# Attention scores of one block as single-pass products of exact float32r halves

## The chip, the cores and the metric

The kernel runs on one core of a Trainium2 chip. The metric is the device time of one execution in microseconds (us). Half a per cent of it is about 27 us.

## The reference, cut to what matters

The input is x (8 sequences of 512 tokens, 256 features) and a context of the same shape. Four residual blocks follow one another: an mLSTM cell over the context, block 2 with attention and experts, block 3 with cross attention, block 4 with a product-key expert layer. The change is in block 2's attention, 32 heads of 8 features each:

```python
xn = (x - mu) / jnp.sqrt(var + 1e-05) * ln_g + ln_b
q = (xn @ wq).reshape(B, S, H, hd)          # H = 32, hd = 8
k = (xn @ wk).reshape(B, S, H, hd)
v = (xn @ wv).reshape(B, S, H, hd)
att = jnp.einsum('bqhd,bkhd->bhqk', q, k) / np.float32(np.sqrt(hd))
p = jax.nn.softmax(att, axis=-1)
o = jnp.einsum('bhqk,bkhd->bqhd', p, v).reshape(B, S, D) @ wo + x
```

Block 3's attention is of the same kind with 16 heads of 16 features. All of it is float32.

## The kernel before

**Phases.** `attention_phase` holds blocks 1 to 3, sequence by sequence (136 to about 3432 us in the trace below), `scores_phase` the queries and key scores of block 4, and the rest of the kernel block 4's experts. The change is in the first phase alone.

**Attention jobs.** There are 24 jobs of 16 heads each: for each of the eight sequences m two jobs of block 2, ("A", m, 0) and ("A", m, 1), which share out its 32 heads, and one of block 3, ("C", m, 0). They run in the order A0 A1 of sequence 0, then for each next m A0, A1 and C of m - 1, at last C of the last (L698). Each job has two passes of 16 steps, and each step two halves:

- *maxima* (L274): for two heads, scores of 128 queries against all 512 keys go to PSUM (`sc`, two banks), and DVE reduces them to the negated maximum (L282). After 16 steps `close_maxima` (L288) transposes the maxima, and four DMAs write them into row 17 of each head's 32-row group of `qa`.
- *exponentials* (L302): the same scores the other way round, keys on the partitions. Row 17 of `ka` is all ones, so the product already has the maximum subtracted. ACT takes the exponential (L310); a step later `values` (L316) multiplies it with v (L324).

`qa` and `ka` are [128, 4, 512]: four row groups of 32 partitions, one for each of four heads that TensorE works on side by side, and four such sets g. Of the 32 rows a block 2 head uses 8 (features) and row 17; the other rows of ka are zero. There are three pairs, two for block 2 (f = 0, 1) and one for block 3. `pair` (L259) issues a product for each of two row groups (L265).

**Order of the work.** The main loop (L798) pairs, in each half, a maxima step of one job with an exponentials step of an earlier one, and issues the products in turn: maxima, exponentials, maxima, exponentials. A job's exponentials begin at least LAG = 2 ticks after its maxima are closed. The two share PSUM through `ps_sc` with two buffers, so that the next maxima products wait for DVE's L282, and the next exponentials for ACT's L310. After each half, `beside` (L774) lets two lanes of other work go on, up to a credit of 1.25 per half; what they yield is their estimated cost. Lane 1 does per sequence the loads, the cell (L379), `queries` (L525) and `values0`; lane 2 the experts, block 3's `operands` and `values1`, and `leave`. The framework may move instructions within each engine's stream by its own estimate; each engine then works in that order.

**Queries and keys of block 2.** `queries` normalises, transposes to `nT`, and projects (L536) into PSUM. ACT scales queries by 1/sqrt(8) (L539), DVE copies keys (L541). The results go to DRAM (`qk_d`, L542) and come back by `spread` (L233): four DMAs of 64 KB for each of qa and ka, each to 8 partitions. `blank` (L242) sets row 17 of qa to zero. Both wait until the previous sequence's job with the same f is done ("rest"). These DMAs go out on SP's queue, as do the maxima's (L298), the cell's `nM_d` (L424) and `mb` (L445), and x's stores.

**Start.** POOL fills the three pairs of qa and ka (L159, L160), then v0, v1 and cte, and then issues the first loads (L363). SP writes the rows of ones into ka (L168).

Of the kernel before, what the change touches and what calls it, by code (L numbers as in the profile page):

```python
# [9 lines left out]

F32 = mybir.dt.float32
U32 = mybir.dt.uint32
U16 = mybir.dt.uint16
U8 = mybir.dt.uint8
# [6 lines left out]
P = 128  # L21
# [13 lines left out]
def kernel(  # L35
# [65 lines left out]
    def attention_phase(ctx: ExitStack):  # L101
# [50 lines left out]

        sets = []
        for i in range(3):
            qa = cst.tile([P, 4, S], F32, name=f"qa{i}")
            ka = cst.tile([P, 4, S], F32, name=f"ka{i}")
            nc.gpsimd.memset(qa, 1.0)  # L159
            nc.gpsimd.memset(ka, 0.0)  # L160
            sets.append((qa, ka))
        ones_d = drm.tile([4, S], F32, name="ones_d", bufs=1)
        nc.sync.dma_start(ones_d.rearrange("(o g) s -> o g s", o=1), sets[0][0][0:1])
        zero_d = drm.tile([4, S], F32, name="zero_d", bufs=1)
        nc.sync.dma_start(zero_d.rearrange("(o g) s -> o g s", o=1), sets[0][1][0:1])
        for i in range(3):
            for j in range(4):
                nc.sync.dma_start(  # L168
                    sets[i][1][32 * j + 17 : 32 * j + 18, :, :],
                    ones_d.rearrange("(o g) s -> o g s", o=1),  # L170
                )


        W0, W1, WC = 32 * 9 + 23, 16 * 17 + 15, 8 * 33 + 31
# [7 lines left out]

        m_u8 = cst.tile([B * NC, P], U8, name="m_u8")
        nc.sync.dma_start(m_u8, mask)
        m_f = cst.tile([B * NC, P], F32, name="m_f")
        nc.vector.tensor_copy(m_f, m_u8)
        mp = ps_m.tile([P, S], F32, name="mp", tag="m")
        nc.tensor.transpose(mp[:, : B * NC], m_f, ident[: B * NC, : B * NC])
# [53 lines left out]
        def blank(qa):  # L242

            for j in range(4):
                nc.sync.dma_start(
                    qa[32 * j + 17 : 32 * j + 18, :, :],
                    zero_d.rearrange("(o g) s -> o g s", o=1),
                )

        class Attention:
            def __init__(self, m, qa, ka, va, first, hd):
                self.m, self.qa, self.ka, self.va = m, qa, ka, va
                self.first, self.hd = first, hd
                self.o = None

            def pair(self, lhs, rhs, g, c, jj):  # L259

                sc = ps_sc.tile([P, 2, S], F32, name="sc", tag="sc")

                def product(i):
                    r = 32 * (2 * jj + i)
                    nc.tensor.matmul(  # L265
                        sc[:, i, :],
                        lhs[r : r + 32, g, c * P : (c + 1) * P],
                        rhs[r : r + 32, g, :],
                        start=True, stop=True,
                    )  # L270

                return sc, product

            def maxima(self, n, half):  # L274

                g, c = n // NC, n % NC
                if n == 0 and half == 0:
                    self.nm = small.tile([P, NC, 4, 4], F32, name="nm")
                sc, product = self.pair(self.qa, self.ka, g, c, half)

                def then():
                    nc.vector.tensor_reduce(  # L282
                        self.nm[:, c, 2 * half : 2 * half + 2, g], sc, AX.X, ALU.max, negate=True
                    )

                return product, then

            def close_maxima(self):  # L288
                nmT = ps_m.tile([P, S], F32, name="nmT", tag="m")
                for c in range(NC):  # L290
                    nc.tensor.transpose(
                        nmT[:16, c * P : (c + 1) * P],
                        self.nm[:, c].rearrange("p j g -> p (j g)"), ident,
                    )
                nm_sb = row.tile([16, S], F32, name="nm_sb")
                nc.any.tensor_copy(nm_sb, nmT[:16])
                for j in range(4):
                    nc.sync.dma_start(  # L298
                        self.qa[32 * j + 17 : 32 * j + 18, :, :], nm_sb[4 * j : 4 * j + 4, :]
                    )  # L300

            def exponentials(self, n, half):  # L302
                g, c, jj = n // NC, n % NC, 1 - half
                if half == 0:
                    self.pr = [None, None]
                sc, product = self.pair(self.ka, self.qa, g, c, jj)

                def then():
                    self.pr[jj] = prb.tile([P, 2, S], F32, name="pr", tag="pr")
                    nc.scalar.activation(self.pr[jj], sc, AF.Exp)  # L310
                    if half == 1:
                        self.ready = (n, self.pr)

                return product, then
# [64 lines left out]
        def cell(m):  # L379
# [30 lines left out]
            nc.scalar.activation(e, e, AF.Exp, scale=-1.0)  # L410
            nc.scalar.activation(e, e, AF.Ln, bias=1.0)
            nc.vector.scalar_tensor_tensor(z, z, 0.0, e, ALU.min, ALU.subtract)
            cs = row.tile([8, S], F32, name="cs")
            nc.vector.tensor_tensor_scan(
                cs, ones[:8, 0:1].to_broadcast([8, S]), z, 0.0, ALU.mult, ALU.add
            )
# [108 lines left out]
        def queries(m):  # L525
            xn = tok.tile([P, NC, D], F32, name="xn", tag="t1")
            lnx[m] = layernorm(xn, xbs[m], keep=3)
            yield 0.3
            layernorm(xn, xn)
            yield 0.3  # L530
            nT = nTs[m] = trp.tile([P, NK, S], F32, name="nT", tag="nT")
            yield from to_features(nT, xn, affine=True)
            pds = [drm.tile([D, S], F32, name="qk_d", bufs=4) for _ in range(2)]
            for i in range(2):
                for n in range(NK):
                    ps = project_T(w0_sb[:, i], nT, n)  # L536
                    pk = trp.tile([P, S], F32, name="pk", tag="pk", bufs=2)
                    if i == 0:
                        nc.scalar.mul(pk, ps, 1.0 / math.sqrt(8.0))  # L539
                    else:  # L540
                        nc.vector.tensor_copy(pk, ps)  # L541
                    nc.sync.dma_start(pds[i][n * P : (n + 1) * P], pk)  # L542
                    yield 1.8
            for f in range(2):
                yield ("rest", ("A", m - 1, f))
                for i in range(2):
                    spread(sets[f][i], pds[i], 32 * f, 8)
                blank(sets[f][0])
                ready.add(("A", m, f))

        def values0(m):
# [75 lines left out]
        def operands(m):  # L627
# [5 lines left out]
            yield 0.3  # L633
            nT = trp.tile([P, NK, S], F32, name="nT3", tag="l2")
            yield from to_features(nT, xn)
            q1, k1 = sets[2]
            for i, srcT, dst in ((1, cT, k1), (0, nT, q1)):
                pd = drm.tile([D, S], F32, name="qk_d3")
                for n in range(NK):
# [148 lines left out]
        def operator(job):  # L788
            kind, m, f = job
            if kind == "A":  # L790
                return Attention(m, *sets[f], v0, 32 * f, 8)
            return Attention(m, *sets[2], v1, 0, 16)

        live, closed = {}, {}
        steps = [(job, n) for job in jobs for n in range(16)]
# [2 lines left out]
        while i2 < len(steps) or pending:  # L798
# [15 lines left out]
            for half in range(2):  # L814
# [2 lines left out]
                    work.append(live[one[0]].maxima(one[1], half))  # L817
                if two:
                    work.append(live[two[0]].exponentials(two[1], half))
                for i in range(2):  # L820
                    for product, _ in work:
                        product(i)
                for _, then in work:
                    then()
                if half == 0 and pending:
# [312 lines left out]
```

## Time and profile before

| | us |
|---|---|
| time, median of 3 runs | 5445.48 (5443.02 to 5463.35) |
| span of the profiled execution, first to last instruction | 5446.6 |
| PE busy in the span | 4895.7 (90%) |
| DVE busy | 2645.6 (49%) |
| ACT busy | 1768.4 (32%) |
| score products (L265), the two directions, PE busy | 1188.9 and 1029.3 |
| maxima (L282), DVE busy | 936.4 |
| exponentials (L310), ACT busy | 781.9 |

PE is TensorE's matmul, PEld its weight load, DVE VectorE, ACT ScalarE, POOL GpSimd, SP SyncE, which here only issues DMAs. A group's line gives the source line, the engine, the operation, output and inputs, shape and count, then busy time and the mean of one in ns, then the idle time just before them and what ended it. The chain is the work that ended last, followed back from the end, each step to what released it. PEclk is the granted clock of TensorE, as a share of full speed; its record knows full and half alone here. The profile gives no time of that execution beside the span.

### The profile page before, as it was taken

The numbers are of one execution on the slowest core, as the hardware profiler recorded it, in microseconds if no ns is written. First come the engines' busy times: TensorE is split into PE (matmuls) and PEld (weight loads), VectorE is DVE, ScalarE is ACT, GpSimd is POOL, SyncE is SP. The second block draws the span as 40 slices with busy tenths as digits, with TensorE's granted clock in tenths as the row PEclk, the third lists the DMA queues.
The fourth block names the chain that finished last, engine by engine and source line by source line (L and its number), as shares of the span: only waits on it lengthen the run. The fifth ranks groups of instructions, "written<-read, shape, count | busy, mean of one in ns | idle before, by whom it ended". The sixth has DMA issues, their size and how long they took to land.

```text
span 5446.6 us, 66461 instructions
## 1 busy us (share of the span) xinstructions
PE 4895.7 (90%) x27301; PEld 2702.6 (50%) x27301; DVE 2645.6 (49%) x5993; ACT 1768.4 (32%) x2314; POOL 232.0 (4%) x321
## 2 busy tenths in 40 slices
PE   6977898888888898888888788799999999999999
PEld 2322333223223233233233232466888888888888
DVE  3443344454453454454454413377855555555543
ACT  2133433344444344344344341355211111111110
POOL 3000010000000000000000000000000000000000
PEclk6688988789889889899889996899888888888887
DMA  2100011100101101111111001200111111111110
GB/s 82 31 17 5 28 50 44 32 28 21 47 25 35 44 28 37 36 32 36 32 24 40 16 17 24 99 1 5 61 45 55 42 53 51 40 58 43 43 52 10
DMA packets 96044, 200.24 MB, mean 37 GB/s; under 512 B 11310, under 2 KB 25934, under 8 KB 95246
## 3 DMA queue, kind: packets, MB, share of 16 engines
q1 hardware_dynamic: 79356, 142.69, 9.1%
q0 software_dynamic: 13056, 46.16, 2.7%
q10 hardware_dynamic: 3328, 7.13, 0.4%
q8 instruction: 215, 3.52, 0.3%
q14 instruction: 89, 0.73, 0.0%
HBM read 165.64 MB, written 29.52 MB: 36 GB/s over the span
## 4 chain that ended last, share of the span: by engine, by line
PE 77%; DVE 12%; issue 4%; DMA 3%; ACT 3%; POOL 1%; SPq 0%; POOLq 0%; DVEq 0%; ACTq 0%
PE sc L265 22%; PE cf L1059 10%; DVE nm L282 9%; PE ps_hd L1032 9%; PE acc L1070 9%; PE av L324 5%; PE ps_pq L883 4%; PE ps_sim L906 2%; PE csc L478 2%; PE ps_p L217 2%; PE ps_y L614 2%; PE ps_q L227 2%; PE cav L455 2%; PE ps_h L595 2%; PE ps_t L201 1%
## 5 line engine op out<-in xcount | busy, mean ns | idle before, releaser
L265 PE MATMUL sc<-ka,qa 32*128 32x512 f32 x3072 | 1188.9, 749 | 313.8 <-DVE nm L282 296.9
L282 DVE TENSOR_REDUCE nm<-sc 128x2 f32<-128x1024 f32 x768 | 936.4, 1223 | 979.4 <-PE sc L265 971.2
L310 ACT ACTIVATE pr<-sc 128x1024 f32<-128x1024 f32 x768 | 781.9, 1023 | 1196.6 <-PE sc L265 1194.6
L265 PE MATMUL sc<-qa,ka 32*128 32x512 f32 x3072 | 1029.3, 734 | 24.1 <-ACT pr L310 11.2
L265 PEld LDWEIGHTS sc<-ka,qa 32*128 32x128 f32 x3072 | 326.2, 211 | 927.7 <-DVE nm L282 759.5
L1032 PE MATMUL ps_hd<-xT,dw 128*128 128x256 f32 x2048 | 573.4, 440 | 14.0 <-ACT gs L1036 7.6
L1059 PEld LDWEIGHTS cf<-m,m 64*128 64x128 f32 x8192 | 560.4, 220 | 35.8 <-issue 31.1
L1059 PE MATMUL cf<-m,m 64*128 64x32 f32 x8192 | 571.9, 302 | 4.0 <-DVE m L1053 4.0
L324 PE MATMUL av<-pr,v 128*32 128x512 f32 x3072 | 485.2, 697 | 41.2 <-ACT pr L310 41.1
L1032 PEld LDWEIGHTS ps_hd<-xT,dw 128*128 128x128 f32 x2048 | 442.4, 222 | 97.3 <-issue 12.3
L1070 PE MATMUL acc<-up_sb,gs 128*128 128x256 f32 x2048 | 474.6, 393 | 2.1 <-DVE gs L1064 1.3
L1036 ACT ACTIVATE gs<-ps_hd 128x512 f32<-128x512 f32 x256 | 152.5, 597 | 938.4 <-PE ps_hd L1032 938.4
L1070 PEld LDWEIGHTS acc<-up_sb,gs 128*128 128x128 f32 x2048 | 405.9, 199 | 66.3 <-DVE fin L1076 4.5
L1064 DVE TENSOR_TENSOR gs<-cf,gs 128x1024 f32<-128x1024 f32 x128 | 156.7, 1225 | 476.1 <-PE cf L1059 476.1
L265 PEld LDWEIGHTS sc<-qa,ka 32*128 32x128 f32 x3072 | 273.1, 207 | 178.5 <-issue 94.6
L1044 DVE TENSOR_TENSOR m<-chT,iota 128x2048 f32<-128x2048 f32 x128 | 292.3, 2284 | 1.3 <-ACT chT L1021 0.9
L324 PEld LDWEIGHTS av<-pr,v 128*32 128x32 f32 x3072 | 64.8, 114 | 393.0 <-issue 311.9
L883 PE MATMUL ps_pq<-xT,wq 128*128 128x512 f32 x512 | 228.1, 599 | 21.1 <-DMA wq<-in_pwq 21.1
L472 ACT ACTIVATE pd<-mb,aT 128x512 f32<-128x512 f32 (+3 forms) x256 | 130.2, 553 | 239.5 <-PE cav L455 114.1
L478 PE MATMUL csc<-qT,cT 32*128 32x256 f32 (+3 forms) x512 | 192.5, 591 | 7.8 <-DVE pd L485 6.7
L346 DVE RECIPROCAL rc<-ot 128x16 f32<-128x16 f32 x96 | 24.7, 257 | 351.3 <-PE ot L342 351.3
L485 DVE SCALAR_TENSOR_TENSOR pd<-csc,pd 128x512 f32<-128x512 f32 (+3 forms) x256 | 117.1, 485 | 139.6 <-PE csc L478 94.6
(186 smaller groups left out, 4294.8 us busy)
## 6 DMA issues: line engine op xcount, KB each, us to landing
dw<-in_down SPq DMA_DIRECT2D x128, 512.0 KB
w1e<-in_w POOLq DMA_DIRECT2D x16, 1024.0 KB, 5.4
w2e<-in_w POOLq DMA_DIRECT2D x16, 1024.0 KB, 6.2
mb<-nM_d SPq DMA_DIRECT2D x32, 512.0 KB
qk_d<-pk SPq DMA_DIRECT2D x64, 256.0 KB
X<-in_x POOLq DMA_DIRECT2D x8, 512.0 KB, 4.5
cT<-in_cxT POOLq DMA_DIRECT2D x8, 512.0 KB, 4.2
cte<-in_cx POOLq DMA_DIRECT2D x32, 128.0 KB, 3.1
```

The source lines that it names most:

```text
L265: nc.tensor.matmul(sc[:, i, :], lhs[r : r + 32, g, c * P : (c + 1) * P], rhs[r : r + 32, g, :], start=True, stop=True,)
L282: nc.vector.tensor_reduce(self.nm[:, c, 2 * half : 2 * half + 2, g], sc, AX.X, ALU.max, negate=True)
L310: nc.scalar.activation(self.pr[jj], sc, AF.Exp)
L324: nc.tensor.matmul(self.av[32 * j : 32 * j + 32, :], self.va[:, c, h * (self.hd + 1) : h * (self.hd + 1) + 32], pr[j // 2][:, j % 2, :], s ...
L478: nc.tensor.matmul(sc[i][:, s0:], cT[r : r + 32, g, s0 : s0 + P], qT[r : r + 32, g, s0:], start=True, stop=True,)
L883: nc.tensor.matmul(ps, wq[:, k, n * P : (n + 1) * P], xT[:, k, b * S : (b + 1) * S], start=(k == 0), stop=(k == NK - 1),)
L1032: nc.tensor.matmul(ps[:, ii, :], dw[:, k, 2 * i + ii, :], xT[:, k, t0 : t0 + TB], start=(k == 0), stop=(k == NK - 1),)
L1036: nc.scalar.activation(g[:, l0 + 2 * i : l0 + 2 * i + 2, :], ps, AF.Gelu_apprx_tanh)
L1044: nc.vector.tensor_tensor(m1, at[:, 0].unsqueeze(2).to_broadcast([P, 16, P]), iota.unsqueeze(1).to_broadcast([P, 16, P]), ALU.is_equal,)
L1059: nc.tensor.matmul(cf[:, h, s, :], m1[64 * h : 64 * h + 64, s, :], m2[64 * h : 64 * h + 64, s, :], start=True, stop=True,)
L1064: nc.vector.tensor_tensor(gv, cf.rearrange("p h s l -> p l h s"), gv, ALU.mult)
L1070: nc.tensor.matmul(acc, g[:, j, c0 : c0 + P], up_sb[:, j, :], start=(j == 0), stop=(j == NJ - 1))
```

## The change

1. **Halves.** Each projected query and key is split into a float32r part (ACT's rounding copy) and the float32r rest (a DVE subtraction); both go to DRAM. The four row blocks of 8 in a head's row group take hi, hi, lo, lo of the query and hi, lo, hi, lo of the key, so that one product over 32 rows sums all four partial products. `spread_halves` does this with 32 DMAs of 64 KB per job, where `spread` had 8; `blank` is no longer called for these jobs.
2. **Maxima.** They no longer sit in row 17. `close_maxima` splits them too, and eight DMAs write them to an own tile `mx[f]`, 8 rows in each row group. The exponentials add a second, accumulating product of 8 rows: `pick`, which selects the set g, times `mx`.
3. **Scale.** 1/sqrt(8) moves from the queries into the exponential's scale.
4. **Order.** The main loop now issues the products term by term: all first terms, then the second ones. Block 3's jobs keep float32 products with one term.
5. **Memory.** The two block 2 pairs are float32r and are not filled at the start; the third pair is filled as before. `nT` shares a buffer with `qT`, `m_f` and `cs` with `e`, and `nm_sb` with the maxima's lo half.

```diff
-        for i in range(3):
-            qa = cst.tile([P, 4, S], F32, name=f"qa{i}")
-            ka = cst.tile([P, 4, S], F32, name=f"ka{i}")
-            nc.gpsimd.memset(qa, 1.0)
-            nc.gpsimd.memset(ka, 0.0)
-            sets.append((qa, ka))
+        def operand_tile(name):
+            return cst.tile([P, 4, S], F32R, name=name)
+        sets = [(operand_tile(f"qa{f}"), operand_tile(f"ka{f}")) for f in range(2)]
+        q1 = cst.tile([P, 4, S], F32, name="q1")
+        k1 = cst.tile([P, 4, S], F32, name="k1")
+        nc.gpsimd.memset(q1, 1.0)
+        nc.gpsimd.memset(k1, 0.0)
...
+        mx = [cst.tile([P, S], F32R, name=f"mx{f}") for f in range(2)]
+        p4 = cst.tile([P, 4], F32, name="p4")
+        nc.vector.tensor_reduce(p4, ident.rearrange("p (m g) -> p g m", g=4), AX.X, ALU.add)
+        pick = cst.tile([P, 4], F32R, name="pick_g")
+        nc.vector.tensor_copy(pick, p4)
...
+        def spread_halves(dst, src, first, halves):
+            for j in range(4):
+                r = j * 64 + first
+                for u, half in enumerate(halves):
+                    at = 32 * j + 8 * u
+                    nc.sync.dma_start(
+                        dst[at : at + 8].bitcast(F32),
+                        src[half, r : r + 32].rearrange("(g d) s -> d g s", d=8),
+                    )
+
+        def halve(dst, ps, n):
+            hi = trp.tile([P, S], F32R, name="pk_h", tag="pk", bufs=2)
+            nc.scalar.copy(hi, ps)
+            lo = trp.tile([P, S], F32R, name="pk_l", tag="pk_l")
+            nc.vector.tensor_tensor(lo, ps, hi.bitcast(F32), ALU.subtract)
+            nc.sync.dma_start(dst[0, n * P : (n + 1) * P], hi.bitcast(F32))
+            nc.sync.dma_start(dst[1, n * P : (n + 1) * P], lo.bitcast(F32))
...
-                def product(i):
+                def product(n, i):
+                    if n >= len(terms):
+                        return
                     r = 32 * (2 * jj + i)
+                    lhs, rhs, rows = terms[n]
                     nc.tensor.matmul(
-                        sc[:, i, :],
-                        lhs[r : r + 32, g, c * P : (c + 1) * P],
-                        rhs[r : r + 32, g, :],
-                        start=True, stop=True,
+                        sc[:, i, :], lhs[r : r + rows], rhs[r : r + rows],
+                        start=(n == 0), stop=(n == len(terms) - 1),
                     )
...
+                hi = row.tile([16, S], F32R, name="nm_h")
+                nc.scalar.copy(hi, nmT[:16])
+                lo = row.tile([16, S], F32R, name="nm_l")
+                nc.vector.tensor_tensor(lo, nmT[:16], hi.bitcast(F32), ALU.subtract)
                 for j in range(4):
-                    nc.sync.dma_start(
-                        self.qa[32 * j + 17 : 32 * j + 18, :, :], nm_sb[4 * j : 4 * j + 4, :]
-                    )
+                    for u, part in enumerate((hi, lo)):
+                        at = 32 * j + 4 * u
+                        nc.sync.dma_start(
+                            mx[self.f][at : at + 4].bitcast(F32),
+                            part[4 * j : 4 * j + 4].bitcast(F32),
+                        )
...
+                terms = [(self.ka[:, g, c * P : (c + 1) * P], self.qa[:, g, :], 32)]
+                if self.hd == 8:
+                    terms.append((pick[:, g : g + 1].to_broadcast([P, P]), mx[self.f], 8))
...
-                    ps = project_T(w0_sb[:, i], nT, n)
-                    pk = trp.tile([P, S], F32, name="pk", tag="pk", bufs=2)
-                    if i == 0:
-                        nc.scalar.mul(pk, ps, 1.0 / math.sqrt(8.0))
-                    else:
-                        nc.vector.tensor_copy(pk, ps)
-                    nc.sync.dma_start(pds[i][n * P : (n + 1) * P], pk)
+                    halve(pds[i], project_T(w0_sb[:, i], nT, n), n)
                     yield 1.8
             for f in range(2):
                 yield ("rest", ("A", m - 1, f))
-                for i in range(2):
-                    spread(sets[f][i], pds[i], 32 * f, 8)
-                blank(sets[f][0])
+                spread_halves(sets[f][0], pds[0], 32 * f, (0, 0, 1, 1))
+                spread_halves(sets[f][1], pds[1], 32 * f, (0, 1, 0, 1))
                 ready.add(("A", m, f))
...
-                for i in range(2):
-                    for product, _ in work:
-                        product(i)
+                for n in range(2):
+                    for i in range(2):
+                        for product, _ in work:
+                            product(n, i)
```

## The prediction

> **What bounds the kernel now.** The span is 5446.6 us, the median of the timed runs 5445.48, so sums made against the span hold for the median within 1 us. The change touches only the attention phase (136 to 3432 us), so I read first the page's chain and groups, then the phase stretch by stretch.
>
> ```profile
> PEclk6688988789889889899889996899888888888887
> PE 77%; DVE 12%; issue 4%; DMA 3%; ACT 3%; POOL 1%; SPq 0%; POOLq 0%; DVEq 0%; ACTq 0%
> L265 PE MATMUL sc<-ka,qa 32*128 32x512 f32 x3072 | 1188.9, 749 | 313.8 <-DVE nm L282 296.9
> L282 DVE TENSOR_REDUCE nm<-sc 128x2 f32<-128x1024 f32 x768 | 936.4, 1223 | 979.4 <-PE sc L265 971.2
> ```
>
> See two things. Each score product is two matmul instructions (3072 for 768 half steps of two products). And the chain goes PE, DVE, PE: a burst of products, the maximum over it, the next burst. L282 holds 9.2% of the chain, 501 us; at 1.23 us each that is some 406 of 768 half steps (53%) in which the next burst waits for the maximum; in the others PE itself is late.
>
> What a burst costs stands in the order of time (start, length, what), first with four products, then a cold one, then one product alone:
>
> ```profile
> 2395.95 0.69 PE L265 MATMUL sc<-ka,qa 32*128 32x512 f32 x1 [0.86 <-DVE nm L282]
> ...
> 2396.50 0.59 PE L265 MATMUL sc<-qa,ka 32*128 32x512 f32 x1
> 2397.02 1.07 PE L324 MATMUL av<-pr,v 128*32 128x512 f32 x8
> ...
> 2398.32 1.12 PE L265 MATMUL sc<-ka,qa 32*128 32x512 f32 x2 [0.23 <-ACT pr L310]
> ...
> 2402.34 1.22 PE L265 MATMUL sc<-qa,ka 32*128 32x512 f32 x1 [2.90 <-DVE nm L282]
> ```
>
> Four products take 1.07 us (2395.95 to 2397.02), one alone 1.12: the four row groups work side by side, and a burst costs what its longest row group costs. Between a group's first and second instruction lie 0.53 us at full clock and 1.02 at half. The part that doubles is 0.48 (two passes), the fixed part 0.05.
>
> The clock is the other half of the matter. The windows view gives length, busy time of PE, PEld, DVE, ACT, POOL, then the granted clock, DMA share and GB/s:
>
> ```profile
> 4020.00:4026.00 6.00, 6.00 (x80) 6.00 (x79) 2.09 (x4) 0.00 (x0) 0.00 (x0) 0.69 0.01 3
> 4030.00:4042.00 12.00, 12.00 (x57) 10.58 (x56) 1.15 (x6) 0.00 (x0) 0.00 (x0) 1.00 0.12 42
> 2054.00:2160.00 106.00, 91.55 (x510) 38.34 (x514) 42.62 (x44) 53.21 (x62) 3.98 (x7) 0.98 0.07 22
> 2160.00:2292.00 132.00, 114.73 (x512) 37.36 (x505) 66.31 (x99) 49.29 (x54) 10.06 (x9) 0.86 0.16 52
> 2292.00:2446.00 154.00, 137.35 (x658) 50.19 (x654) 77.93 (x148) 66.28 (x90) 13.07 (x22) 0.86 0.12 29
> ```
>
> In the first two PE is busy without a gap, yet 64x32 products (L1059) run at 0.69 and 128x128 products at 1.00. So I weighed each matmul record by its share of the array (rows times columns) and its array time, and summed over the clock record's steps of 3.41 us. Of 618 steps in the attention phase filled to over 39% of what the full clock allows, all 618 are followed by full clock; of 199 filled under 31%, 18 are. **The clock follows how full the array is.** The last three rows are one block's cycle: A maxima beside C exponentials (S1), A beside A (S2), C maxima beside A exponentials (S3).
>
> **What the change saves on PE.** A float32r product should be one instruction of one pass. No row has one. Bounds: as dear as a full float32 instruction, 0.53; or half its array time, 0.24 + 0.05 = 0.29. I take 0.29 (0.53 at half clock), since the array time is the larger part. A's maxima then cost 0.29, its exponentials two products on the same row group, 0.58. By pairing the job list, 288 half steps have A on both sides (9 jobs), 192 are A maxima beside C, 224 C maxima beside A, 32 the first job alone.
>
> - A beside A: PE saves 1.07 - 0.58 = 0.49; where the maximum is waited for it saves 1.07 - 0.29 = 0.78. At 53% this is 0.64 x 288 = 184 us of full-clock work.
> - A maxima beside C: the C burst keeps 1.07, so ACT's exponential (1.02) becomes the wait in place of DVE's 1.23: some 0.15 x 0.68 (L282 is 26.7 of 106 us of S1's chain) x 192 = 20 us.
> - C maxima beside A: nothing. The second product runs on its own row group under C's 1.07. If it queued behind instead, 0.29 x 224 = 65 us are lost; the four starts within 20 ns speak for zero.
> - The first job alone: (1.07 - 0.29) x 32 = 25 us.
>
> Together 229 us of full-clock work.
>
> **What the clock takes back.** Laying the chain on the clock record, the phase holds 1456 us of PE at full clock, 774 at half (share c = 0.347), and 1066 of everything else. At full clock the PE part is 1456 + 774/2 = 1843. After the change PE needs (1843 - 229)/(1 - c/2) = 1614/(1 - c/2):
> c = 0.347 gives 1953 (277 less than 2230); 0.45 gives 2083 (-147); 0.52 gives 2181 (-49); 0.60 gives 2306 (+76). It breaks even at 0.55.
> Single passes fill the array less. With an instruction of 0.48 counted as two passes of 512 columns, an A job's 128 products on a quarter of the array each fill it for 65.5 thousand columns; after the change (64 x 128 for maxima, 64 x 160 for exponentials with their 8-row product) 18.4 thousand. That is a fifth of the phase's fill. Taking just that out of each step, those under 37.5% (between the two bounds above) rise from 32% to 53% at unchanged time, to 45% if all runs 1.1 times denser; half clock holds 29% of the phase now. Scaled as now (0.347/0.29) that is c = 0.54 to 0.63. Faster half steps in S2 fill steps again once they are warm, so I take c = 0.52: **-49 us**.
>
> The Trainium skill (TensorE: Matmul & The Clock Gate, Part 1) has the clock fall to half after an idle window of about 3.4 us, and says to avoid PE gaps over some 3 us. By that rule PE, still busy, would keep its clock, and the PE term would be the -277 of c = 0.347. The first windows row speaks against it: no gap, 0.69.
>
> **What the transfers add.** Spreading goes from 8 transfers of 64 KB and 4 of blanks per A job to 32 of 64 KB, 2 MB for 0.5.
>
> ```profile
> 2431.90 1.46 SPq L237 DMA_DIRECT2D ka<-qk_d  x4
> 2433.45 1.31 SPq L237 DMA_DIRECT2D qa<-qk_d  x4
> 2435.24 3.45 SPq L237 DMA_DIRECT2D ka<-qk_d  x4
> ```
>
> Two pieces of the chain (start, length, what), at block 1 and at the start of the kernel:
>
> ```profile
> 398.69 6.40 DMA qa<-zero_d
> ```
> ```profile
> 8.24 1.75 POOL qa L159
> ```
>
> Four issues take 1.3 to 1.5 us until the queue is full, then 3.45; the packets landing from 2435 to 2445 carry 50 to 80 KB per us, so a spread costs about 1 us. In this block the first transfer goes out at 2420.5, the last that the next A job's maxima need at 2433, and PE comes to that job at 2444.96, 8 us after it landed. With 24 of 32 needed for the first half step, 2420.5 + 24 + 3 = 2448, and 2456 for the second: 3 to 11, I take 8 us late in each of 6 blocks, 48 (0 to 120). PE is in order: av, values and C's exponentials stand behind those maxima. The second set's 32 end some 70 us before their use. At the start the 64 transfers from 141.5 last to about 205; the next cell's nM and mb, now issued at 166.5 and 168, are behind them on SP, and its sums behind those on PE: 25 (0 to 37), 5 for the first maxima. Block 1 has its spread on the chain already (the 398.69 piece): 24 more transfers, 20 (10 to 30). Sum **+98** (10 to 190).
>
> **Small terms.** Four of six memsets of 1.75 us go from ahead of the first load on POOL: **-7** (0 to -7). Halving adds per block two ACT copies (0.59) and two DVE passes (0.69), and makes DVE wait for ACT's copy, which can stand behind an exponential; the next L282 is queued behind it. 6 such places x 8 blocks x 0.3 = **+15** (0 to 58, at 1.2 each). Maxima closing has 8 transfers for 4, about 3 us, under the 12 us that lie between landing and use where A's set 1 of block 3 closes (1504 to 1516). The scale is a field of the same ACT instruction. The buffers now shared (qT and nT; m_f, e and cs; nm_sb and lo) are used one after the other on their engines already: 0.
>
> Sum: -49 + 98 - 7 + 15 = +57: 5446.6 + 57, about **5505 us**.
>
> **Rivals.**
> 1. The forecast: passes saved, clock cooler, transfers late: 5505 (5475 to 5580). For it: S2 and S3 already stand at 0.86. Chance 0.42.
> 2. Faster: the denser A steps keep the clock near c = 0.40: 1614/0.80 = 2018, -212, with the +106 of the other terms about 5340; with c at 0.347 and transfers at their lower end, 5190. It decides where S2 keeps a clock of 0.80. Against it: S2 is left with 70% of its fill. Chance 0.28.
> 3. Even: c about 0.48 (1614/0.76 = 2124, -106) and the transfers as above cancel: 5445. Chance 0.13.
> 4. The clock collapses: in S2 and S3 a cold step can't be filled to the threshold any more, c = 0.66: 1614/0.67 = 2409, +179 + 106, about 5730. It decides from c = 0.55 up. Chance 0.12.
> 5. It doesn't do what it says: a float32r product costs the full 0.53. A beside A then saves PE nothing and the maximum's path 0.54 at 53%, 82 us, the first job 17: 1744/(1 - c/2), at c = 0.45 2250 (+20), with the +106 of the rest 5570. Against it: nothing in this trace; it decides if the two products of an A exponential stand 0.5 us apart. Chance 0.05.
>
> **Numbers.** Slower takes 1, 4 and 5: 0.59; a difference under 0.5% (27 us), about what a measurement here can tell from none, 0.13; faster 0.28. Both signs hold most of the chance; the range from 5290 to 5690 leaves out the low end of rival 2 and most of 4.
>
> **What would show it.** L265 in float32r form with about 0.3 us between products of a group; S2's granted clock under 0.75 and S3's under 0.80; L265 waiting for DMA qa or ka at each new block, with 3.5 us per four L237 issues. A clock of 0.85 in S2 would prove me wrong towards rival 2; L265 starting new blocks without a DMA wait would remove the +98.

## The result, and the profile after

The changed kernel takes 5519.6 us (median of 4 runs, 5503.23 to 5537.16); the kernel before, on the same chip, 5448.02 (5443.02 to 5463.35). The ratio is 1.0139, 95% interval 1.0103 to 1.0176: slower by 1.4%, and the forecast of 5505 us lies 15 us under it. The profiled execution of the changed kernel has a span of 5535.2 us, 88.6 more than the one of before.

First the page of the changed kernel: the clock by slices, the chain by engine, then the groups that answer to the two shown of before (L265 is now L306, L282 is L323), and the added product.

```profile
PEclk6565896677877767767767777899888888898987
...
PE 77%; DVE 9%; DMA 5%; ACT 4%; issue 3%; POOL 1%; SPq 0%; POOLq 0%; ACTq 0%; DVEq 0%
...
L323 DVE TENSOR_REDUCE nm<-sc 128x2 f32<-128x1024 f32 x768 | 933.3, 1222 | 1005.7 <-PE sc L306 986.2
...
L306 PE MATMUL sc<-ka,qa 32*128 32x512 f32 x1024 | 364.3, 636 | 197.0 <-DVE nm L323 137.7
...
L306 PE MATMUL sc<-mx,pick_g 8*128 8x512 f32 x1024 | 288.1, 514 | 7.6 <-DMA mx<-nm_l 7.6
```

Each score product of block 2 is now one instruction: of the 3072 of the group before, 1024 were block 3's, whose operands now have a group of their own, and half of the other 2048 were second instructions. The clock's digits for the attention phase, the first 25 or so, are mostly sixes and sevens where eights stood. DVE has gone from 12% of the chain to 9%, DMA from 3% to 5%.

The products in order of time, first at full clock, then at half (start, length, what):

```profile
2644.22 0.50 PE L306 MATMUL sc<-ka,qa 32*128 32x512 f32 x2
2644.23 0.50 PE L306 MATMUL sc<-qa,ka 32*128 32x512 f32 x2
2644.57 0.40 PE L306 MATMUL sc<-mx,pick_g 8*128 8x512 f32 x2
2644.89 0.64 PE L384 MATMUL av<-pr,v 128*32 128x512 f32 x4
...
2655.89 0.79 PE L306 MATMUL sc<-qa,ka 32*128 32x512 f32 x2
2656.48 0.63 PE L306 MATMUL sc<-mx,pick_g 8*128 8x512 f32 x2
```

Four first products start within 10 ns, the second ones 0.34 us later, the values 0.67 us after the first. So a float32r product is one instruction and takes some 0.33 us, where the two float32 instructions of a product took 1.07. At half clock the same step is 0.59 us (2655.89 to 2656.48), so the part that doubles is 0.26, about half of a float32 instruction's 0.48: one pass for two.

The windows view of the same block as in the prediction, whose three jobs now end at 2200, 2315 and 2495 us (length, busy PE, PEld, DVE, ACT, POOL, granted clock, DMA share, GB/s):

```profile
2074.00:2200.00 126.00, 111.27 (x444) 44.03 (x444) 42.54 (x43) 53.73 (x61) 3.98 (x7) 0.77 0.19 37
2200.00:2315.00 115.00, 94.84 (x452) 37.09 (x450) 66.33 (x102) 52.68 (x58) 9.96 (x9) 0.84 0.19 56
2315.00:2495.00 180.00, 161.63 (x654) 57.77 (x652) 79.34 (x151) 68.88 (x93) 13.03 (x22) 0.67 0.14 38
```

Beside the clocks of before (0.98, 0.86, 0.86): only the middle stretch, A beside A, got shorter, 132 to 115 us, and it kept its clock. The two stretches in which block 3's float32 products share the burst got longer, 106 to 126 and 154 to 180, at 0.77 and 0.67. This block flatters the middle stretch. Over the six stretches of its kind from the third sequence on, each got shorter (790 us together before, 700 after), but their mean clock fell from 0.85 to 0.79.

Where did the time go? I laid the chain of each trace on its clock record, from 136 us to the end of the attention phase. "Work" is the PE part of the chain as it would be at full clock, c the share of the PE part that lies at half clock.

| | half clock, share of the phase | PE work | c | PE part | everything else |
|---|---|---|---|---|---|
| before | 0.29 | 1843 | 0.347 | 2230 | 1067 |
| after | 0.53 | 1605 | 0.600 | 2292 | 1097 |

238 us of full-clock work are gone, and the clock takes them back and 62 more. It takes them from the neighbours: the score products fall from 1180 to 985 us of the chain, while av goes from 260 to 408, csc and cav (block 3's cell) from 146 to 237. In "everything else" the changes nearly cancel. Waits of the next burst for the maximum fall from 500 to 370 us, and transfers of mb from 55 to 8; transfers of the queries and keys (qa and ka) rise from 10 to 124, those of the maxima from 2 to 24, and the exponentials (ACT) from 69 to 106. The phase ends 93 us later; what follows it keeps its length within 5 us.

### The profile page after: what moved, and what is told of

Same layout as the page of the kernel before. It is cut to its first block, busy times and chain, and to the rows that moved or that the text cites. A ratio compares the mean times of both kernels' runs of the same rounds, so it can differ in the third digit from the quotient of the medians.

```text
span 5535.2 us, 64942 instructions
## 1 busy us (share of the span) xinstructions
PE 4971.5 (90%) x26277; PEld 2781.0 (50%) x26277; DVE 2646.0 (48%) x6028; ACT 1814.9 (33%) x2357; POOL 223.5 (4%) x317
## 4 chain that ended last, share of the span: by engine, by line
PE 77%; DVE 9%; DMA 5%; ACT 4%; issue 3%; POOL 1%; SPq 0%; POOLq 0%; ACTq 0%; DVEq 0%
PE sc L306 18%; PE cf L1112 10%; PE ps_hd L1085 9%; PE acc L1123 8%; PE av L384 7%; DVE nm L323 7%; PE ps_pq L936 4%; PE csc L538 3%; PE cav L515 3%; PE ps_p L234 3%; PE ps_sim L959 2%; PE ps_h L648 2%; ACT pr L367 2%; PE ps_q L244 2%; PE ps_y L667 2%
## 5 line engine op out<-in xcount | busy, mean ns | idle before, releaser
L323 DVE TENSOR_REDUCE nm<-sc 128x2 f32<-128x1024 f32 x768 | 933.3, 1222 | 1005.7 <-PE sc L306 986.2
L384 PE MATMUL av<-pr,v 128*32 128x512 f32 x3072 | 561.2, 797 | 41.7 <-ACT pr L367 41.2
L306 PE MATMUL sc<-k,q 32*128 32x512 f32 x1024 | 474.0, 922 | 83.8 <-DVE nm L323 82.0
L306 PE MATMUL sc<-ka,qa 32*128 32x512 f32 x1024 | 364.3, 636 | 197.0 <-DVE nm L323 137.7
L306 PEld LDWEIGHTS sc<-ka,qa 32*128 32x128 f32 x1024 | 135.8, 228 | 619.1 <-DVE nm L323 332.2
L306 PE MATMUL sc<-q,k 32*128 32x512 f32 x1024 | 381.9, 811 | 31.4 <-DMA q<-nm_sb 17.4
L306 PE MATMUL sc<-qa,ka 32*128 32x512 f32 x1024 | 340.6, 634 | 38.9 <-ACT pr L367 19.5
L306 PEld LDWEIGHTS sc<-k,q 32*128 32x128 f32 x1024 | 125.9, 256 | 340.0 <-DVE nm L323 263.2
L306 PE MATMUL sc<-mx,pick_g 8*128 8x512 f32 x1024 | 288.1, 514 | 7.6 <-DMA mx<-nm_l 7.6
L538 PE MATMUL csc<-qT,cT 32*128 32x256 f32 (+3 forms) x512 | 214.9, 666 | 10.7 <-DVE pd L545 9.5
```

The source lines that it names most:

```text
L306: nc.tensor.matmul(sc[:, i, :], lhs[r : r + rows], rhs[r : r + rows], start=(n == 0), stop=(n == len(terms) - 1),)
L323: nc.vector.tensor_reduce(self.nm[:, c, 2 * half : 2 * half + 2, g], sc, AX.X, ALU.max, negate=True)
L384: nc.tensor.matmul(self.av[32 * j : 32 * j + 32, :], self.va[:, c, h * (self.hd + 1) : h * (self.hd + 1) + 32], pr[j // 2][:, j % 2, :], s ...
L538: nc.tensor.matmul(sc[i][:, s0:], cT[r : r + 32, g, s0 : s0 + P], qT[r : r + 32, g, s0:], start=True, stop=True,)
```

## The experiments

Three theories were set against each other. **T1**: how full the array is sets the clock, so that the saved passes are paid for at half clock; the transfers add about 100 us. **T2**: waits, for the transfers above all, cool the clock, and make up the loss. **T3**: only PE's busy time matters.

**The passes alone.** The kernel before with block 2's operands in float32r tiles: no halves, no second product, no added transfers. The operands are rounded to float32r, so the scores aren't the reference's exact ones.

```diff
-            qa = cst.tile([P, 4, S], F32, name=f"qa{i}")
-            ka = cst.tile([P, 4, S], F32, name=f"ka{i}")
+            kind = F32 if i == 2 else F32R
+            qa = cst.tile([P, 4, S], kind, name=f"qa{i}")
+            ka = cst.tile([P, 4, S], kind, name=f"ka{i}")
```

> The kernel before, with block 2's queries and keys in float32r tiles as they are (rounded, without the exact rest): each score product of an A job is one single-pass product, and nothing else is changed: no 32-transfer spread, no second product, no halving. Theory 1 (the array is filled less and the clock falls): full-clock work of PE in the attention phase falls by about 250 us to some 1590, its half-clock share rises from 0.35 to about 0.60, and 1590/0.70 = 2270 against 2230 leaves nothing of the gain: 5440 to 5520 us, mean clock of the run under 0.80. Theory 2 (the loss came from the transfers, and the clock fell only because PE waited for them): without them the saved passes show, 5160 to 5250 us, clock about 0.85.

Measured: 5373.48 us, ratio 0.9866 (0.9843 to 0.989), clock 0.785.

```profile
PEclk6656887878677777678677596898888888888887
PE 81%; ACT 8%; DVE 7%; DMA 2%; issue 2%; POOL 0%; SPq 0%; another core or an unknown queue 0%; ACTq 0%; DVEq 0%; POOLq 0%
```

The clock is that of the changed kernel without one of its transfers, which T2 can't have. The time lies between the two theories: c = 0.576, PE part 2396 us (166 more than before), everything else 830 (237 less, since waits for the maximum fall from 500 to 215). So the single passes do gain, some 70 us, but where the bursts waited, not in PE's time.

**The maxima alone as float32r.** The kernel before, with A's maxima read as float32r; the exponentials stay float32. The maxima are then those of rounded products.

```diff
+                lhs, rhs = self.qa, self.ka
+                if self.hd == 8:
+                    lhs, rhs = lhs.bitcast(F32R), rhs.bitcast(F32R)
-                sc, product = self.pair(self.qa, self.ka, g, c, half)
+                sc, product = self.pair(lhs, rhs, g, c, half)
```

> The kernel before, with only the maxima products of block 2 read as float32r (rounded, no exact rest); exponentials stay float32, transfers as before. In a half step with A on both sides the float32 exponentials still hold PE for 1.07 us, so PE is relieved of hardly anything, but the array's fill falls by 64 x 384 = 24.6 thousand columns per A job, half of what the whole change takes away. Theory 1 (fill sets the clock): half-clock share of the attention phase 0.38 to 0.45, mean clock 0.81 to 0.83, and the time is no better than before: 5440 to 5560 us. Theory 2 (the clock falls where PE waits for transfers or other engines): clock 0.85 as before, and the shorter way to the maximum shows: 5340 to 5420 us.

Measured: 5610.32 us, ratio 1.0289 (1.0257 to 1.032), clock 0.804. This edit only takes work out of the array, and the kernel is slower by 2.9%. A burst beside float32 exponentials keeps its length (row groups work side by side), so PE's work falls by 26 us only, to 1817; but c rises to 0.539 and the PE part from 2230 to 2486 us. It is T1's strongest support, in sign; T1 had its size too small by 50 us.

The windows view, 300 to 3400 us and, for contrast, 4200 to 5300 us in block 4's experts, of the kernel before, then of this run:

```profile
300.00:3400.00 3100.00, 2673.91 (x12662) 966.20 (x12658) 1368.71 (x2055) 1244.53 (x1500) 177.42 (x241) 0.87 0.11 30
4200.00:5300.00 1100.00, 1096.29 (x8540) 971.06 (x8538) 587.08 (x1214) 175.94 (x282) 0.00 (x0) 0.87 0.16 48
```
```profile
300.00:3400.00 3100.00, 2729.53 (x11083) 959.54 (x11080) 1312.07 (x1985) 1208.05 (x1433) 168.62 (x233) 0.78 0.10 29
4200.00:5300.00 1100.00, 1095.79 (x8546) 972.23 (x8544) 606.79 (x1320) 179.65 (x286) 0.00 (x0) 0.87 0.16 48
```

PE is no less busy (2730 us for 2674), yet its clock is 0.78 for 0.87; the untouched stretch keeps 0.87.

**The transfers alone, twice.** First each spread was issued four times to the same rows:

```diff
-                nc.sync.dma_start(
+                for _ in range(4 if hd == 8 else 1):
+                    nc.sync.dma_start(
```

> The kernel before, with every spread transfer of block 2 issued four times (32 per job, the same 64 KB each, the result is the same). Theory 1: transfers alone cost 60 to 130 us, as each new A job waits for them: 5505 to 5575 us, while the clock stays at 0.84 to 0.86, since the products fill the array as before. Theory 2: they pull the clock down as well, to 0.80 or less.

Measured: 5709.08 us, ratio 1.0507 (1.0481 to 1.0534), clock 0.844; 421 us of the chain are transfers. The size missed: transfers to the same rows follow one another more closely than the change's (SyncE waits 540 us in all for earlier spreads before it issues the next; in the changed kernel 177). So a second run sends the 24 further transfers of each job to rows of a tile that nobody reads, with the buffers shared as in the changed kernel:

```diff
+                if hd == 8:
+                    for u in range(3):
+                        at = 32 * j + 8 * (u + 1)
+                        nc.sync.dma_start(
+                            spare4[at : at + 8],
+                            src[r : r + 4 * hd].rearrange("(g d) s -> d g s", d=hd),
+                        )
```

> The kernel before, with 24 further spread transfers per job of block 2 into a tile that nothing reads (32 in all, 64 KB each), none behind another to the same place as in the run of transfers issued four times; to make room, nT shares qT's buffer and m_f and cs share e's, as in the kernel after. Theory 1: the late transfers alone cost about what the prediction's sum gave, 60 to 150 us, 5505 to 5600 us, at an unchanged clock of 0.84 to 0.86. Theory 2: the clock falls too, under 0.82.

Measured: 5548.99 us, ratio 1.0175 (1.014 to 1.0211): 105 us more than before, where the prediction put 98. The clock is 0.842, the phase's share at half clock 0.34. In the same window as above (300 to 3400 us):

```profile
300.00:3400.00 3100.00, 2663.68 (x12361) 959.41 (x12360) 1328.05 (x2015) 1229.74 (x1485) 180.29 (x245) 0.85 0.14 37
```

The transfers cost what they were forecast to. They do cool the clock a little: the share at half clock goes from 0.29 to 0.34, a fifth of the rise to 0.53 in the changed kernel, and here nobody waits for the added rows themselves. But the passes alone bring the clock all the way down without any added transfer, so as the account of the low clock **T2 falls.**

The other way about, the changed kernel with 8 of its 32 spreads per job; the three further blocks of 8 rows are zeros, so that the scores are of first halves alone.

```diff
-                for u, half in enumerate(halves):
+                for u, half in enumerate(halves[:1]):
```

> The kernel after, with 8 of the 32 spread transfers per job: only the first 8 rows of each group are brought in, the others stay zero from a fill at the start (four memsets more on POOL, 7 us), so that scores are those of the rounded halves alone; all products and maxima are as in the kernel after. Theory 1: the transfer pieces leave the chain (124 us of q and k in the kernel after, some 25 remain), the clock stays as low as after: 5400 to 5460 us, clock 0.78 to 0.80. Theory 2 (transfers cause the low clock): clock back to 0.84 or more and 5150 to 5300 us.

Measured: 5434.62 us, ratio 0.9975 (0.9946 to 1.0004), clock 0.791, c = 0.589. Taking most of the transfers out wins 85 us against the changed kernel, and next to no clock (c was 0.600).

Where they stand in the changed kernel, at the start of one block in the chain (start, length, what):

```profile
2475.89 3.15 DMA qa<-qk_d
...
2479.05 5.99 DMA qa<-qk_d
...
2485.06 5.97 DMA ka<-qk_d
...
2491.05 5.97 DMA ka<-qk_d
...
2497.26 2.10 PE sc L306 x5
```

21 us in which the chain is on the spreads, before a burst that then runs at half clock.

**Filling the array with more work.** Two runs put a further product into each burst of the changed kernel, between first products, with 128 and with 32 stationary columns; what it writes is overwritten.

```diff
+                    if n == 0 and len(terms) == 2 and i == 0:
+                        nc.tensor.matmul(
+                            sc[:128, i, :], lhs[:, :128], rhs, start=True, stop=True
+                        )
```

> The kernel after, with one product more in each half step of an A job's exponentials: 128 rows by 128 columns by 512, float32r, written to PSUM where the real product then starts over it. It is pure extra work, 512 products of about 0.25 us. Theory 1: it raises PE's full-clock work by about 130 us to 1735 but fills the array, so the half-clock share falls from 0.60 to about 0.45: 1735/0.775 = 2239 against 2292, some 50 us faster than the kernel after: 5420 to 5520 us, clock 0.81 or more. Theory 3 (PE only has to be busy, what it does doesn't matter): the added work adds to the time, 5620 to 5720 us.

> The control to the run with the added 128x128 product: the same added product, but of 32 columns of the array in place of 128, so that PE is kept as long and a quarter as many cells work. Theory 1: the clock hardly rises (half-clock share 0.57), 1735/0.715 = 2427 against 2292, some 130 us slower than the kernel after: 5600 to 5720 us, clock under 0.79. Theory 3: the same time as with 128 columns.

Measured: 6331.35 us (ratio 1.1631, 1.1609 to 1.1654) and 6280.09 (1.1548, 1.1525 to 1.1572). Both miss by far and tell nothing of T1: with a product over all 128 rows between two products on row groups, the groups no longer run side by side. In the chain of the first (start, length, what), L307 is the added product:

```profile
2700.84 0.51 PE sc L310 x2
2701.35 0.43 PE sc L307
2701.78 0.66 PE sc L310 x4
```

What had been a burst of 0.67 us is 1.6. Two further runs put the product at the front of the burst:

```diff
+                def fill():
+                    if self.hd == 8:
+                        for _ in range(1):
+                            nc.tensor.matmul(
+                                sc[:128, 0, :], self.ka[:, g, c * P : c * P + 128],
+                                self.qa[:, g, :], start=True, stop=True,
+                            )
...
+                    live[two[0]].fill()
```

> The kernel after, with the added 128x128 product of 512 columns put ahead of the burst of each half step with A exponentials (it had stood between the products and broken up their row groups), where PE mostly waits for the maximum; the real product then starts over it. Theory 1: 512 products of 0.33 us, half of them in PE's waits, add some 90 us of full-clock work, but the half-clock share falls from 0.60 to about 0.50 of the chain's PE time: 1695/0.75 = 2260 against 2292, 5430 to 5530 us, clock 0.80 or more. Theory 3 (only busy time matters): slower than after by 60 to 170 us with no higher clock.

> The changed kernel with one further float32r product of block 2 at the front of every exponential half's burst, as in the run with 128 stationary columns there (5722 us, 0.562 of the matmul part of the chain at half clock, work at full clock 1853 us), but with 32 columns: the same instructions, a quarter of the array filled by them. T1 (the array's fill sets the clock): the same work, 0.60 or more at half clock, so 5730 to 5800 us. T2 (waits for transfers) and T3 (busy time alone): the same as with 128 columns, 5700 to 5745 us and 0.55 to 0.57.

Measured: 5722.16 us (1.0498, 1.045 to 1.0546) with 128 columns and 5596.67 (1.0286, 1.0252 to 1.0321) with 32. With 128, c falls from 0.600 to 0.562 as T1 has it, but the work rises by 248 us, 0.48 for each of the 512 products. With 32, the work rises by 179 and c falls further, to 0.543: against T1's expectation and against the two others'. The added product by itself, first with 128, then with 32 columns (min/median/max in ns):

```profile
L368 PE MATMUL sc<-qa,ka x512: 473/505/802, 221.3 to 3434.5; 128*128 128x512 f32 x171
```
```profile
L368 PE MATMUL sc<-qa,ka x512: 414/424/1415, 224.6 to 3358.8; 128*32 128x512 f32 x171
```

The narrow product is the shorter one, and the clock stays at least as high. Counted by rows times columns, the steps of the 32-column run don't separate as they do in all other runs (of 122 filled 31 to 35%, 50 are followed by full clock; in the changed kernel 4 of 100). With its columns counted three to four times, as if the unused ones worked too, they do (9 of 111, 5 of 99). So here the unused columns seem to count; no run was made for that alone.

**Filling it with the same work.** The changed kernel with more of the array in use by instructions that are there anyway: the product that carries the maximum takes 32 rows, 24 of them zeros, and the gate's products 112 stationary columns.

```diff
+        for one_mx in mx:
+            nc.gpsimd.memset(one_mx.bitcast(F32), 0.0)
...
-                    terms.append((pick[:, g : g + 1].to_broadcast([P, P]), mx[self.f], 8))
+                    terms.append((pick[:, g : g + 1].to_broadcast([P, P]), mx[self.f], 32))
...
-                        gp[:8], gw_sb[:, k, 8 * i : 8 * i + 8],
+                        gp[:112], gw_w[:, 16 * k + 8 * i : 16 * k + 8 * i + 112],
```

> The changed kernel with more of the array filled by the same instructions: the product that carries the maximum contracts over 32 rows, 24 of them zeros, in place of 8, and the gate's products hold 112 stationary columns, of which 8 count, in place of 8. T1: the share at half clock falls from 0.60 to 0.50 to 0.57 and the time from about 5520 us to 5400 to 5490 us, at a mean clock over 0.795. T2 and T3: 5500 to 5535 us, clock 0.785.

Measured: 5471.61 us, ratio 1.0057 (1.0032 to 1.0083), where the changed kernel had 1.0139 (1.0103 to 1.0176): a gain of some 45 us from the same instructions. c falls to 0.536 and the PE part by 144 us, to 2148.

```profile
PEclk6666986777778777777877787999898888888887
```

This is T1's forecast in sign and size, and neither T2 nor T3 has a place for it. Which of the two parts won it, the next run asks.

**The gate's columns by themselves**, on the run with the passes alone (whose operands are rounded):

```diff
-                        gp[:8], gw_sb[:, k, 8 * i : 8 * i + 8],
+                        gp[:112], gw_w[:, 16 * k + 8 * i : 16 * k + 8 * i + 112],
```

> The run that had the single passes alone (block 2's operands rounded to float32r, so that the scores aren't the reference's exact ones; 5373 us), with the gate's products holding 112 stationary columns in place of 8. T1: a lower share at half clock than 0.576 and 5290 to 5370 us. T2 and T3: 5365 to 5380 us.

Measured: 5385.3 us, ratio 0.989 (0.9861 to 0.9919), beside 0.9866 (0.9843 to 0.989) without it: nothing gained, c 0.579 for 0.576. T1 missed here. So the gain of the run before most likely came from the added rows of zeros; they were not tried without the columns. What the columns are worth is taken up with the steps of the clock below.

**Two queues.** The run with free fill, with half of the spreads on GpSimd's queue:

```diff
-                    nc.sync.dma_start(
+                    (nc.sync if u < 2 else nc.gpsimd).dma_start(
```

> The run before it in this list, with half of the spreads of each job (u of 2 and 3) issued on GpSimd's queue in place of SyncE's. The trace of the changed kernel has 124 us of the chain on transfers of qa and ka, about 6 us each, three in a row at a new block. If the queue sets that time, two queues halve it: 40 to 70 us less than the run before it. If the rows that all the transfers share set it, or the issues on GpSimd stand behind its other work, 0 to 20 us less, or more. Every theory agrees on the clock: as in the run before it.

Measured: 5419.02 us, ratio 0.9959 (0.9935 to 0.9983), as expected if the queue sets the time: 53 us less than without the second queue, and the first version with the full computation that is faster than the kernel before, by 0.4%. Transfers of qa and ka take 78 us of the chain where they took 181.

```profile
PE 77%; DVE 11%; DMA 5%; ACT 5%; issue 2%; POOL 1%; SPq 0%; another core or an unknown queue 0%; DVEq 0%; POOLq 0%; ACTq 0%
...
L310 PE MATMUL sc<-ka,qa 32*128 32x512 f32 x1024 | 355.0, 616 | 176.1 <-DVE nm L327 136.5
```

**The steps of the clock, run by run.** As in the prediction, each trace's matmuls were summed over the steps of 3.41 us, a float32r product as one pass, from 172 us to the end of the phase:

| | steps filled over 39%, followed by full clock | under 31%, followed by full clock | mean fill |
|---|---|---|---|
| before | 620 of 620 | 19 of 211 | 0.49 |
| after | 357 of 357 | 30 of 409 | 0.38 |
| passes alone | 335 of 335 | 40 of 444 | 0.36 |
| transfers alone (unused rows) | 592 of 592 | 17 of 264 | 0.47 |
| free fill | 444 of 444 | 5 of 327 | 0.42 |
| free fill, two queues | 447 of 447 | 9 of 310 | 0.43 |

The rule read from the trace of before holds in every one of these; what the change does is to take nearly half of the steps away that pass it (620 to 357). The stretch counted differs a little from the prediction's, so its counts (618 and 18 of 199) do too.

The same traces tell rows from columns, if each product is spread evenly over its recorded time and the one threshold is taken that puts the fewest steps on the wrong side. By rows times columns 58 of the changed kernel's 984 steps are wrong, by rows alone 227, by PE's busy share 357 (before: 36, 97 and 240 of 957); the order is the same in every run. So columns do count, and T3's measure is the worst. The exceptions come mostly from one product: with the gate's eight columns counted as the whole 128, the 58 fall to 29 and before's 36 to 16, and of before's steps under 31% none of 185 is then followed by full clock. The values products, 32 columns each and four side by side, must be counted as they stand (four times as wide, 245 are wrong). It looks as if a narrow product that has the rows to itself counts as the whole width. Then widening the gate's operand could win nothing, as the run above found. This is read off the traces; no run was made for it.

## Why the prediction was right

**The work on PE.** Forecast 229 us saved, to 1614; the trace has 1605. A float32r product was taken as 0.29 us, the low end of its bounds; it is 0.33, and the pair of an exponential 0.67 for 0.58. Both are small errors. A's second product does run under C's burst, as assumed (start, length, what; q and k are block 3's operands):

```profile
2346.33 0.69 PE L306 MATMUL sc<-k,q 32*128 32x512 f32 x1
2346.34 0.50 PE L306 MATMUL sc<-qa,ka 32*128 32x512 f32 x1
...
2346.68 0.40 PE L306 MATMUL sc<-mx,pick_g 8*128 8x512 f32 x2
2346.86 0.60 PE L306 MATMUL sc<-k,q 32*128 32x512 f32 x2
2347.39 0.44 PE L515 MATMUL cav<-pd,cte 128*64 128x128 f32 x4
```

The burst still takes 1.06 us (2346.33 to 2347.39).

**The clock.** This was the mechanism, and its size is the step that missed. The count of steps gave 53% of the phase at half clock; the trace has 0.529. Scaled, that gave c = 0.54 to 0.63; I then took 0.52, since "faster half steps in S2 fill steps again". In S2 of the block shown they do (0.84, and 17 us shorter, where I had said under 0.75), less so over the six (0.79); but S1 fell to 0.77 and S3 to 0.67, which the discount forgot: there the burst still lasts as long as C's float32 products, with less in it. At 0.60 the prediction's own formula gives +76 us; measured +62. The rival of a collapse was priced at c = 0.66 and said to decide from 0.55; c did pass that point, and the shorter waits for the maximum kept the time from it. The faster rival's sign, S2 at 0.80 or more, was there in the block shown and just missed over all six, but its time did not come.

The Trainium skill (TensorE: Matmul & The Clock Gate, Part 1) names as cause an idle window of about 3.4 us. Of the 521 steps that are followed by half clock in the changed kernel, 33 touch a gap of PE of over 3 us, and 218 have under 0.1 us of idle time in all. The rule may account for places such as the 21 us shown above, not for the phase.

**The transfers.** +98 forecast. By themselves they cost 105 us, and taking most of them out of the changed kernel wins 85. A spread costs about 0.72 us, a little under the 1 us assumed; SyncE issues the 16 of ka in 11.49 us:

```profile
2482.81 11.49 SPq L273 DMA_DIRECT2D ka<-qk_d  x16
```

The eight transfers of the maxima, which the sum put at nothing, hold 24 us of the chain.

**The start and the small terms** were not tried apart. The first maxima start 14 us later (185.8 for 172.0 us); the first job's take 38 us for 103, the second's 200 for 133. In that stretch (136 to 424 us) 130 of the 155 us of PE in the chain lie at half clock, csc and cav first (70 us), and 15 us are transfers of qa and ka. The third job starts 16 us later than before, the sixth 17 earlier. The forecast had -25 for the first job, +50 for the start and block 1, +8 for memsets and halving, so some 30 us in all; the trace has 16 by the third job, and shows that part of it is again the clock.

**What was not foreseen** is that "everything else" rose by 30 us and not by 106. The waits for the maximum fell by 130 us. I had counted what the shorter path to the maximum saves as PE work; it also ends in the waits, largely because a PE at half clock is late more often than DVE. Before, 581 maxima ended at full clock and had 433 us of the chain, 187 at half clock and had 66; after, 397 of the 768 end at half clock. At the rates of before that alone makes some 84 of the 130 us. So an error of 111 us on the clock (+62 for -49) was met by one of 76 on the rest, and the sum came out 15 us short of the median (30 short of the profiled span). That is luck: the mechanism was right, but the sum is better than its terms.

## What to carry to other kernels

Fewer passes on a partly filled array can lower the clock for everything that runs beside them: weigh what a stretch would fill after the change, stretch by stretch, before counting the saved time. If a product must be made smaller, rows of zeros in instructions that are there anyway may win some of the clock back; products added for that purpose cost more than they win, between products on row groups most of all. And more transfers into the operands cost their landing time wherever a block begins; a second queue took more than half of that away.

## What had not been expected of the hardware

- Taking half of the passes out of the maxima alone made the kernel 2.9% slower (5610 us), with PE as busy as before.
- A product over all 128 rows costs far more between products on single row groups than its own 0.42 to 0.50 us: some 810 us for 512 of them (6331 for 5520 us), 200 us at the front of the burst.
- Widening the stationary operand from 8 to 112 columns left the clock where it was (c 0.576 and 0.579); widening the contraction from 8 to 32 rows, with the gate's columns, took c from 0.600 to 0.536. In the count of steps the 8-column product weighs as much as one of 128 columns, while products of 32 columns side by side weigh only what they fill; a run for that alone is missing.
